# Second attention of a two-layer kernel: side work cut at engine changes, one transposition for the maxima, two engines' sums added before the ones-product

## The chip, the cores and the metric

One Trainium2 chip; the program runs on one of its cores. The metric is the device time of the whole program in microseconds, of which the profile shows one execution.

## The reference, cut to what matters

Two layers on `x` of (4, 512, 256), each a cross attention to a context of 1601 rows and then a mixture of 8 experts. The change is in layer 1: its attention, and the routing of its experts that runs beside it.

```python
# layer 1 attention: h = layernorm(x), 8 heads of 32, keys and values from the context
q = split(h @ Wq.T); k = split(ctx @ Wk.T); v = split(ctx @ Wv.T)
attn = softmax(einsum('bhnd,bhmd->bhnm', q, k) * 32**-0.5)
x = x + merge(einsum('bhnm,bhmd->bhnd', attn, v))
# layer 1 experts: h = layernorm(x)
logits = h @ Wr + br
thresh = top2(logits)[1]
weights = softmax(where(logits >= thresh, logits, -inf))
out = sum_e weights[e] * (gelu(h @ W1[e] + b1[e]) @ W2[e] + b2[e])
x = x + out
```

The shift that a softmax subtracts (the maximum of a row) cancels in the quotient.

## The kernel before, in words

There are four stages in time: the first attention (to about 1577 us), the first experts (to about 1937), the second attention (to about 2606), the second experts (to the end). Every product is float32 on TensorE, and a float32 matmul shows as two records, a transposition as one.

**Second attention.** Its work is cut into 16 units u = (batch b of 4, group o of four heads, half f of the queries), 256 queries of four heads each. A unit has NM = 13 steps j over the 1601 keys, 128 at a time, so step 13u + j; a batch has 52 steps. The outer loop makes an *iteration* of two steps, and writes this order out by hand (`in_order` fixes the order on TensorE, VectorE, ScalarE and GpSimd):

- `weights` of each of the two steps: scores, transposed (keys on partitions), into `ps_w` (L1357), then the exponential on ScalarE into `pT` (L1370). Between the two steps stands one piece of `maxima` of the unit after: scores with queries on partitions into `ps_s` (L1109), and VectorE's maximum of them into `tops` (L1120). A unit has seven such pieces.
- `add_weights` of the two steps before: `sum += pT` (L1379), on GpSimd for j in (1, 4, 7, 10) and on VectorE else, into two sums. Step 0 and step 1 write theirs directly, so GpSimd has three adds per unit and VectorE eight.
- `weigh` of the two steps before: `ps_o += v * pT` (L1388). After the last step of a unit `closing` copies `ps_o` to `oT` (L1400); two iterations later it sums over keys with a product with ones (`ps_n`, L1407, one set of matmuls for each of the two sums); an iteration later it turns `oT` back and divides.
- whatever was put down for these steps by `put`: the side work.

How the maximum gets into the scores: `keyed` and `asked` have 64 rows for a pair of heads, of which 32 hold keys and queries, and one more row of `keyed` holds ones (row 32, and 96 for the other head) while the same row of `asked` holds the negative maxima of the queries. `negated(u)` (L1129) writes them into `shift`, at step 13u-5; `to_row(u)` turns `shift` with four transpositions (L1142) and copies two rows of 512 into `asked` (L1146), at step 13u-4. For an odd u these steps are in one iteration, for an even u in two.

**Side work in this stage.** `collect` gathers the first experts' results for batch b + 1 (8 indirect loads on GpSimd) and `add_collected` adds them; `queries` makes batch b + 1's layer norm and queries; `projected` (batches 1 and 2) makes keys and values of batch b + 1, a piece per iteration, with ScalarE copying them out; `route2(b - 1)` makes the routing of the second experts for the batch before: layer norm, logits, the two chosen experts, their places, the biases' product, and at the end 16 indirect stores ("scatters") of 128 rows of `pay` into `rows_a` and `rows_b` on GpSimd (L535). `queries` and `route2` are generators; each `next` runs one piece. In `ln_root` (L133, L135) VectorE adds the epsilon and ScalarE takes the square root, which takes a table load (and another back to the exponential's).

**Buffers.** `ps_s`, 3 buffers of two banks, serves `ps_w`, the two `ps_s` tiles of a maxima piece and all side work's products; `ps_o` has 1; `ps_m` has 1 and serves `ps_n`, the turned outputs and `ps_r`. `pT` has 6 buffers.

**First experts, second half.** `all_experts(1, keys_next())` calls `next` on the generator `keys_next` twice per expert and once at the end. Its pieces are the projections of batch 1, `queries(0)`, the seven maxima of unit 0, and last `negated(0)` with `to_row(0)`.

**Second experts.** The generator `routing` (`route2(3)` and a table) is called four times per expert tile in `for i in range(E + SURE)`.

Of the kernel before, what the change touches and what calls it, by code (L numbers as in the profile page):

```python
# [16 lines left out]
P = 128  # L17
# [53 lines left out]
def xattn_ffn_twice(ctx: ExitStack, tc: tile.TileContext, a: dict, out: bass.AP):  # L71
# [42 lines left out]
    def ln_moments(pool, src, n, tail=P, mv=None, some=None):  # L114

        if mv is None:
            mv = pool.tile([P, n, 2], F32, tag=f"mv{n}", name="mv")
            if tail < P:
                nc.vector.memset(mv, 1.0)
        for i in some or range(n):  # L120
            r = rows_of(i, n, tail)
            st = pool.tile([P, 6], F32, tag="bnst", name="st")
            nc.vector.bn_stats(st[:r], src[:r, i, :])
            nc.vector.bn_aggr(mv[:r, i, :], st[:r])
        return mv
# [5 lines left out]
    def ln_root(pool, mv, n):  # L131
        ve = pool.tile([P, n], F32, tag=f"ve{n}", name="ve")
        nc.vector.tensor_scalar(ve, mv[:, :, 1], EPS, None, ALU.add)  # L133
        rs = pool.tile([P, n], F32, tag=f"rs{n}", name="rs")
        nc.scalar.activation(rs, ve, AF.Sqrt)  # L135
        return ve, rs
# [62 lines left out]
    in_row = const.tile([P, 1], F32, name="in_row")  # L199
    nc.gpsimd.memset(in_row, 0.0)  # L200
    for r in (32, 96):
        nc.gpsimd.memset(in_row[r : r + 1], 1.0)
# [193 lines left out]
    def route2(b, two, psum, tag, first=0, n=NT):  # L396
# [4 lines left out]
        mv = ln_moments(two, xb, n)  # L401
        root = ln_root(two, mv, n)
        yield
        mv, rs = ln_scale(two, mv, n, root)
        for t in range(n):
            nc.vector.tensor_scalar(
                pay[:, t, :D],
                xb[:, t, :],
                mv[:, t, 0:1],
                rs[:, t : t + 1],  # L410
                ALU.subtract,
                ALU.mult,
            )
            nc.vector.tensor_scalar(
                pay[:, t, D : D + 1], lane, float((b * NT + first + t) * P), None, ALU.add
            )
        xnT = two.tile([P, DC, n * P], F32, tag="xnT2", name="xnT2")
        yield
# [30 lines left out]
        nc.vector.tensor_tensor(wb, lg, top[:, :, 0:1].to_broadcast([P, n, E]), ALU.subtract)  # L449
        nc.scalar.activation(wb, wb, AF.Exp)  # L450
# [5 lines left out]
        nc.vector.tensor_copy(pay[:, :, D + 1 :], wb)  # L456

# [3 lines left out]
        for k in range(2):  # L461
# [7 lines left out]
            chosen.append(ck)  # L469
        mine_b = slice(b * NT + first, b * NT + first + n)  # L470
        nc.vector.tensor_reduce(over[:, mine_b], rest, AX.X, ALU.add)
        nc.vector.tensor_tensor(extra[:, mine_b, :], rest, wb, ALU.mult)

# [3 lines left out]
        for t in range(n):  # L477
            nc.vector.tensor_copy(earlier[:, t, :], taken2)
            nc.vector.tensor_tensor(taken2, taken2, cnt[:, t, :], ALU.add)
        ps = psum.tile([P, n, E], F32, tag=tag, name="ps_c2")  # L480
# [7 lines left out]
        if b == B - 2:  # L488
            nc.vector.tensor_copy(taken_a, taken2)
        for k in range(2):  # L490
            off, place, at, out_of = small("off2"), wide("place"), small("at2"), small("out_of")
            nc.vector.tensor_tensor(place, hot[k], ps, ALU.mult)
# [18 lines left out]
        yield  # L511

        tp = psum.tile([P, 4, P], F32, tag=tag, name="tp_w")
        for t in range(n):
            nc.tensor.transpose(tp[:E, t, :], wb[:, t, :], ident)
        wbT = two.tile([E, n * P], F32, tag="wbT", name="wbT")
        nc.vector.tensor_copy(wbT, tp[:E, :n].rearrange("p i q -> p (i q)"))
        for t0 in range(0, n, 2):
            ps = psum.tile([P, 2, D], F32, tag=tag, name="ps_b2")
            for k in range(2):  # L520
                t = t0 + k
                nc.tensor.matmul(
                    ps[:, k, :], lhsT=wbT[:, t * P : (t + 1) * P], rhs=b2, start=True, stop=True
                )
            xs = xb[:, t0 : t0 + 2, :]
            nc.vector.tensor_tensor(xs, xs, ps, ALU.add)
            yield
# [3 lines left out]
        for rows, at in ((rows_a, place_a), (rows_b, place_b))[b == B - 1 :]:  # L531
            for k in range(2):
                for t in range(n):
                    j = b * NT + first + t
                    nc.gpsimd.indirect_dma_start(  # L535
                        out=rows[:, :],
                        out_offset=bass.IndirectOffsetOnAxis(ap=at[k][:, j : j + 1], axis=0),
                        in_=pay[:, t, :],
                        in_offset=None,
                        bounds_check=E * G - 1 if rows is rows_a else ROWS - 1,  # L540
                        oob_is_err=False,
                    )
                    yield


    with ExitStack() as st:
# [339 lines left out]
        nc.gpsimd.memset(empty, 0.0)  # L886
        with in_order(nc.sync):
            load_second()
# [159 lines left out]
    shift = [soon.tile([P, 2, 2, P], F32, name=f"shift{i}") for i in range(2)]  # L1048
# [3 lines left out]
    def queries(b, qT):  # L1052
        xn = soon.tile([P, NT, D], F32, tag="xn", name="xn")
        mv = ln_moments(turns, x[b], NT)
        root = ln_root(turns, mv, NT)
# [4 lines left out]
        yield  # L1060
# [66 lines left out]
    def negated(u):  # L1127
        for pair in range(2):
            nc.vector.tensor_reduce(  # L1129
                shift[u % 2][:, :, pair, 32::64],  # L1130
                tops[u][:, :, 2 * pair : 2 * pair + 2, :],
                AX.X,
                ALU.max,
                negate=True,
            )
        tops.pop(u)

    def to_row(u):
        ps = banks["m"].tile([P, 2, QH], F32, tag="m", name="ps_r")
        for pair in range(2):  # L1140
            for t in range(2):
                nc.tensor.transpose(  # L1142
                    ps[:, pair, t * P : (t + 1) * P], shift[u % 2][:, t, pair, :], ident
                )
        for r in (32, 96):
            nc.scalar.copy(asked[u % 3][r : r + 1], ps[r : r + 1])  # L1146
# [173 lines left out]
    with ExitStack() as st:  # L1320
# [9 lines left out]

        keyed = [one.tile([P, 2, M], F32, name=f"keyed{o}") for o in range(DC)]
        of_ones = ones[:, 0:1].to_broadcast([P, M])
        for t in keyed:
            nc.scalar.activation(t[:, 0], of_ones, AF.Copy, scale=in_row[:, 0:1])
            nc.vector.tensor_scalar(t[:, 1], of_ones, in_row[:, 0:1], None, ALU.mult)

        def load_keys(b, o):
            for pair in range(2):
                for s in range(2):
# [4 lines left out]
                    )  # L1344

# [27 lines left out]
        def add_weights(u, j, pT):  # L1373
# [5 lines left out]
            (nc.gpsimd if k else nc.vector).tensor_tensor(to, to, pT[:r], ALU.add)  # L1379

# [15 lines left out]
        def closing(u, ps):  # L1396
# [7 lines left out]
            for k in range(2):  # L1404
                for i in range(HG):
# [6 lines left out]
                        stop=k == 1,  # L1412
# [30 lines left out]
        n_units, per_batch = len(units), 4 * NM  # L1443
# [31 lines left out]

        for u in range(1, n_units):
            put(NM * u - 5, lambda u=u: negated(u))
            put(NM * u - 4, lambda u=u: to_row(u))
            put(NM * u - 12, lambda u=u: load_queries(u))
        for b in range(B):  # L1480
            s0 = per_batch * b
            if b:
                put(s0 - 10, lambda b=b: load_keys(b, 0))
                put(s0, lambda b=b: load_keys(b, 1))
                spread(s0 + 10, route2(b - 1, one, ps_s, "s"), 2, 24)
            if b + 1 < B:
# [4 lines left out]
                for t in range(NT):  # L1491
                    put(
                        s0 + 14 + 2 * t,
# [6 lines left out]
                spread(s0 + 22, later(), 2, 5)  # L1500
# [26 lines left out]
        held = []  # L1527
        for step in range(0, NM * n_units + 10, 2):

            fresh = []  # L1530
            for k in range(step, step + 2):
# [3 lines left out]
                if k == step:  # L1535
                    for g in ahead.pop(step // 2, ()):
                        maxima(*g)
            for h in held:
                add_weights(*h)
            for uw, jw, pT in held:  # L1540
                if jw == 0:
# [11 lines left out]
        assert not at and not ahead, (sorted(at), sorted(ahead))  # L1553

# [3 lines left out]
    with ExitStack() as st:  # L1558
# [242 lines left out]
        for i in range(E + SURE):  # L1801
            w, xT, to, share = here
            hT = hidden(w, xT)
            for _ in range(2):
# [5 lines left out]
            next(rest, None)  # L1810
            if last:
                results(*last)
            next(rest, None)
# [131 lines left out]
```

## Time and profile before

| what | value |
|---|---|
| median of 3 runs | 2953.87 us (2949.18 to 2956.38) |
| the profiled execution | 2949.11 us |
| its span | 2947.0 us |
| mean granted TensorE clock | 0.973 |
| second attention, from its first `ps_w` to its last `oT` | 1937.7 to 2598.9 us |
| `pT` exponential, 128x1024, each | 1023 ns |
| VectorE's add, alone, and mean of all | 1222 and 1435 ns |
| GpSimd's add, median | 2372 ns |
| one maxima reduction, 128x1024 | 1217 ns |
| scatter, from issue to landing | 3.0 us (`rows_a`), 2.6 us (`rows_b`) |

Times are of one execution, counted from the span's start. "PE" is TensorE's matmuls, "PEld" its weight loads, DVE VectorE, ACT ScalarE, POOL GpSimd, SP SyncE. In a wait "X <- Y" X stood still until Y ended; in order of time a row has its start, its length, the engine, the line, and in brackets the idle time before it and what ended it. "xN" counts instructions.

### The profile page before, as it was taken

To read this page: it belongs to the slowest core of one execution; us is meant where nothing else is said; L and a number is where in the kernel's file an instruction comes from. 1 tells how busy PE (TensorE), PEld (TensorE's weight loads), DVE (VectorE), ACT (ScalarE), POOL (GpSimd) and SP (SyncE) were. 2 spreads that over 40 slices of the span, in tenths; PEclk is the share of its full clock that TensorE was granted. 3 is DMA by queue.
4 is the path that set the end of the run, shared out by engine and by line. 5 is a ranking of instruction groups with operands and counts; after the bars stand their busy time and mean duration, and the time that the engine had idled before them with its cause. 6 is when DMAs were issued, how large, how long until landed. Compare 5 with 4: busy or idle time off the path is not lost. (4 is left out here: it accounts for less than half of the span.)

```text
span 2947.0 us, 36216 instructions
## 1 busy us (share of the span) xinstructions
PE 2770.3 (94%) x13686; PEld 1883.4 (64%) x13686; DVE 1466.2 (50%) x2333; ACT 937.7 (32%) x1325; POOL 392.5 (13%) x301
## 2 busy tenths in 40 slices
PE   6999999999999999999999799988989898889997
PEld 2666667666766666666666587744444444467886
DVE  6445456544575544454444202267767768742110
ACT  3323334233342333332332112134434344331221
POOL 0000000100001000010000101021314233333442
PEclk9999999999999999999999899999999999999999
DMA  5444443343434333343346798610101021035663
GB/s 162 113 108 113 104 112 85 102 106 92 104 98 109 95 91 92 89 109 94 91 99 185 199 255 235 185 46 16 30 28 48 19 66 63 11 114 154 180 188 82
DMA packets 197448, 314.94 MB, mean 107 GB/s; under 512 B 44007, under 2 KB 118056, under 8 KB 194440
## 3 DMA queue, kind: packets, MB, share of 16 engines
q1 hardware_dynamic: 157512, 227.52, 29.1%
q0 software_dynamic: 15168, 49.23, 5.7%
q10 hardware_dynamic: 24576, 35.68, 4.7%
q8 instruction: 114, 1.87, 0.3%
q14 instruction: 78, 0.64, 0.1%
HBM read 114.64 MB, written 51.86 MB: 56 GB/s over the span
## 5 line engine op out<-in xcount | busy, mean ns | idle before, releaser
L806 DVE TENSOR_REDUCE top<-ps_s 128x1 f32<-128x2113 f32 x128 | 301.9, 2358 | 585.2 <-PE ps_s L798 585.2
L835 PE MATMUL ps_o<-pT,v 128*128 128x256 f32 x2176 | 521.1, 381 | 0.5 <-DVE inv L813 0.5
L798 PE MATMUL ps_s<-kT,qT 128*128 128x512 f32 (+1 forms) x1280 | 488.8, 526 | 6.5 <-ACT attn L812 6.4
L835 PEld LDWEIGHTS ps_o<-pT,v 128*128 128x128 f32 x2176 | 410.0, 191 | 114.5 <-issue 68.3
L812 ACT ACTIVATE attn<-ps_s,top 128x2113 f32<-128x2113 f32 x128 | 258.9, 2023 | 477.5 <-DVE top L806 433.2
L798 PEld LDWEIGHTS ps_s<-kT,qT 128*128 128x128 f32 x1280 | 241.8, 191 | 252.9 <-issue 236.5
L827 DVE STREAM_TRANSPOSE pT<-swapped 128x2176 f32<-128x2176 f32 x128 | 312.4, 2441 | 31.0 <-DMA swapped<-attn 20.4
L1120 DVE TENSOR_REDUCE tops<-ps_s 128x2 f32<-128x1024 f32 (+1 forms) x224 | 238.1, 1105 | 149.6 <-PE ps_s L1109 149.2
L747 PE MATMUL ps_k<-kvin,wkv 128*128 128x512 f32 (+1 forms) x640 | 263.8, 535 | 4.1 <-DVE mv_g L685 2.1
L1357 PE MATMUL ps_w<-asked,keyed 64*128 64x256 f32 (+1 forms) x1664 | 244.7, 416 | 21.1 <-DVE tops L1120 9.6
L781 PE MATMUL ps_v<-wkv,kvin 128*128 128x256 f32 x1088 | 254.6, 381 | 0.7 <-ACT v L788 0.6
L1357 PEld LDWEIGHTS ps_w<-asked,keyed 64*128 64x128 f32 (+1 forms) x1664 | 147.5, 190 | 146.6 <-ACT pT L1370 61.8
L1370 ACT ACTIVATE pT<-ps_w 128x1024 f32<-128x1024 f32 (+1 forms) x176 | 179.3, 1023 | 193.7 <-PE ps_w L1357 191.9
L781 PEld LDWEIGHTS ps_v<-wkv,kvin 128*128 128x128 f32 x1088 | 205.0, 190 | 35.9 <-ACT v L788 6.0
L1379 DVE TENSOR_TENSOR sum<-sum,pT 128x1024 f32<-128x1024 f32 (+1 forms) x128 | 183.2, 1431 | 10.4 <-ACT pT L1370 4.0
L760 ACT ACTIVATE kT<-ps_k,bqk 128x512 f32<-128x512 f32 (+1 forms) x160 | 96.8, 620 | 266.5 <-DMA swapped<-attn 129.0
L1379 POOL TENSOR_TENSOR sum<-sum,pT 128x1024 f32<-128x1024 f32 x48 | 122.6, 2554 | 347.5 <-ACT pT L1370 347.3
L747 PEld LDWEIGHTS ps_k<-kvin,wkv 128*128 128x128 f32 x640 | 116.4, 192 | 78.5 <-issue 67.4
L1109 PE MATMUL ps_s<-kv,qT 32*128 32x512 f32 (+1 forms) x1024 | 135.4, 574 | 14.6 <-ACT kv L1013 6.5
L788 ACT COPY v<-ps_v 128x512 f32<-128x512 f32 x144 | 79.7, 560 | 217.0 <-PE ps_v L781 150.2
L1193 PE MATMUL ps_h<-sxT,w 128*128 128x256 f32 x512 | 116.7, 386 | 2.9 <-ACT hT L1200 2.1
L1207 PE MATMUL ps_y<-w,hT 128*128 128x256 f32 x512 | 114.4, 380 | 0.2 <-DVE y L1215 0.2
(282 smaller groups left out, 2731.5 us busy)
## 6 DMA issues: line engine op xcount, KB each, us to landing
swapped<-attn SPq DMA_DIRECT2D x1536, 68.0 KB, 2.1
swapped<-attn ACTq DMA_DIRECT2D x512, 68.0 KB, 2.2
w<-in_w_dram SPq DMA_DIRECT2D x32, 1024.0 KB, 10.2
rows_b<-empty SPq DMA_DIRECT2D x36, 530.0 KB, 11.3
w_e<-in_wall_dram SPq DMA_DIRECT2D x4, 2052.0 KB, 9.3
cw<-in_ctxT_dram SPq DMA_DIRECT2D x4, 1601.0 KB, 12.5
keyed<-kv SPq DMA_DIRECT2D x32, 200.1 KB, 3.8
ctx_b<-in_ctx_dram SPq DMA_DIRECT2D x3, 1536.0 KB, 8.0
```

The source lines that it names most:

```text
L747: nc.tensor.matmul(ps[:, :n], lhsT=wkv[:, c, hs], rhs=kvin[:, c, : NB - 1, k, :] if k < 4 else kvin[:, c, NB - 1, :, :], start=c == 0, sto ...
L781: nc.tensor.matmul(ps[:, k, :], lhsT=flat_kvin[c][:, j * P : (j + 1) * P], rhs=wkv[:, c, cols], start=c == 0, stop=c == DC - 1,)
L798: nc.tensor.matmul(flat[:, j0 : j0 + n], lhsT=qT[:, t * P : (t + 1) * P], rhs=kT[:, j0 : j0 + n], start=True, stop=True,)
L806: nc.vector.tensor_reduce(top, flat[:, :L], AX.X, ALU.max, negate=True)
L812: nc.scalar.activation(attn[:, :L], flat[:, :L], AF.Exp, bias=top, accum_out=total)
L827: nc.vector.transpose(pT[:, :, k * P : (k + 1) * P].rearrange("p c (a i) -> p a c i", a=4), swapped.rearrange("p a (c i) -> p a c i", i=32),)
L835: nc.tensor.matmul(ps, lhsT=v[:, j - parts[part][0], (h % 2) * DH0 : (h % 2 + 1) * DH0], rhs=pT[:, j, :], start=j == 0, stop=j == NB - 1,)
L1109: nc.tensor.matmul(pss[i // 2][:, i % 2, at : at + n], lhsT=qTs[b][rows, o, q0 : q0 + P], rhs=kvs[b][0][o][rows, j0 : j0 + n], start=True, ...
L1120: nc.vector.tensor_reduce(tops[u][:, t : t + at // n, 2 * pair : 2 * pair + 2, j0 // 512], of, AX.X, ALU.max,)
L1357: nc.tensor.matmul(ps[:r, s, pair * QH : (pair + 1) * QH], lhsT=keyed[o][64 * s : 64 * s + 64, pair, j * P : j * P + r], rhs=asked[u % 3][ ...
L1370: nc.scalar.activation(pT[:r], ps[:r], AF.Exp)
L1379: (nc.gpsimd if k else nc.vector).tensor_tensor(to, to, pT[:r], ALU.add)
```

## The change

- `negated(u)` is one reduction instead of two, at step 13u-7; it writes four columns (32 to 35) in each half of a 128x128 `shift`, in the order query tile, pair. `to_row(u)` at 13u-5 is one transposition and four ScalarE copies of four rows each, which a column of `in_row` scales by one or zero; `keyed` has ones in two of these four rows for each pair. `in_row` is made from four small reductions of the identity.
- At a unit's last step GpSimd adds the second sum to the first (all units but the last), and `ps_n` is one set of matmuls.
- When a unit's last step and the next one's first are in one iteration, `weigh` of the first is put off into the next iteration, ahead of its adds.
- `queries` yields ten times instead of five, `route2` in more places: after each part that another engine goes on with. `wbT` is copied by ScalarE, the counts are copied out of PSUM, and scatters go two to a call, the first four beside the biases' product.
- The steps of the calls are written as lists. `add_collected` starts at 10 instead of 14, `queries` at 12 instead of 22, `route2` at 4 instead of 10.
- The second experts call `routing` eight times per tile.

```diff
-        mv = ln_moments(two, xb, n)
-        root = ln_root(two, mv, n)
+        mv = ln_moments(two, xb, n, some=range(n // 2))
+        yield
+        ln_moments(two, xb, n, mv=mv, some=range(n // 2, n))
+        ve = ln_variance(two, mv, n)
+        yield
+        root = ln_root(two, mv, n, ve)
         yield
         mv, rs = ln_scale(two, mv, n, root)
+        yield
...
+        if b == B - 2:
+            nc.vector.tensor_copy(taken_a, taken2)
+        yield
         ps = psum.tile([P, n, E], F32, tag=tag, name="ps_c2")
...
+        counted = two.tile([P, n, E], F32, tag="counted", name="counted")
+        nc.vector.tensor_copy(counted, ps)
+        tp = psum.tile([P, 4, P], F32, tag=tag, name="tp_w")
...
+        nc.scalar.copy(wbT, tp[:E, :n].rearrange("p i q -> p (i q)"))
+        yield
...
+        def scatters():
+            for rows, at in ((rows_a, place_a), (rows_b, place_b))[b == B - 1 :]:
+                for k in range(2):
+                    for t in range(n):
+                        j = b * NT + first + t
+                        nc.gpsimd.indirect_dma_start(
...
+                        if t % 2:
+                            yield
+        sending = scatters()
         for t0 in range(0, n, 2):
...
+            next(sending)
             yield
...
+        yield from sending
...
     def queries(b, qT):
         xn = soon.tile([P, NT, D], F32, tag="xn", name="xn")
-        mv = ln_moments(turns, x[b], NT)
-        root = ln_root(turns, mv, NT)
+        mv = ln_moments(turns, x[b], NT, some=())
+        for i in range(NT):
+            ln_moments(turns, x[b], NT, mv=mv, some=(i,))
+            if i + 1 < NT:
+                yield
+        ve = ln_variance(turns, mv, NT)
+        yield
+        root = ln_root(turns, mv, NT, ve)
         yield
         mv, rs = ln_scale(turns, mv, NT, root)
         for i in range(NT):
             ln_apply(xn, x[b], mv, rs, i)
-        yield
+            if i in (0, NT - 1):
+                yield
...
     def to_row(u):
-        ps = banks["m"].tile([P, 2, QH], F32, tag="m", name="ps_r")
-        for pair in range(2):
+        ps = banks["m"].tile([P, P], F32, tag="m", name="ps_r")
+        nc.tensor.transpose(ps, shift[u % 2], ident)
+        for r in (32, 96):
             for t in range(2):
-                nc.tensor.transpose(
-                    ps[:, pair, t * P : (t + 1) * P], shift[u % 2][:, t, pair, :], ident
-                )
-        for r in (32, 96):
-            nc.scalar.copy(asked[u % 3][r : r + 1], ps[r : r + 1])
+                nc.scalar.activation(
+                    asked[u % 3][r : r + 4, :, t * P : (t + 1) * P],
+                    ps[r : r + 4].unsqueeze(1).to_broadcast([4, 2, P]),
+                    AF.Copy,
+                    scale=in_row[r : r + 4, 2 + t : 3 + t],
+                )
...
             (nc.gpsimd if k else nc.vector).tensor_tensor(to, to, pT[:r], ALU.add)
+            if j == NM - 1 and merged(u):
+                nc.gpsimd.tensor_tensor(sums[u, 0], sums[u, 0], sums[u, 1], ALU.add)
...
         for u in range(1, n_units):
-            put(NM * u - 5, lambda u=u: negated(u))
-            put(NM * u - 4, lambda u=u: to_row(u))
+            put(NM * u - 7, lambda u=u: negated(u))
+            put(NM * u - 5, lambda u=u: to_row(u))
...
-                spread(s0 + 10, route2(b - 1, one, ps_s, "s"), 2, 24)
+                beside = (4, 8, 10, 18, 20, 22, 24, 28, 30, 32, 34, 36, 38, 40, 42, 44, 46)
+                bare = (4, 8, 10, 12, 14, 16, 18, 20, 22, 24, 26, 28, 30, 32, 34, 36, 38)
+                steps = beside if b + 1 < B else bare
+                place(s0, route2(b - 1, one, ps_s, "s"), (*steps, *range(steps[-1] + 2, 54, 2), *range(54, 62)))
...
-                spread(s0 + 22, later(), 2, 5)
+                place(s0, later(), range(12, 32, 2))
...
             for uw, jw, pT in held:
+                if jw == 0 and held and held[0][:2] == (uw - 1, NM - 1):
+                    late = [(uw, jw, pT)]
+                    continue
```

## The prediction

> **What bounds the kernel now.** I read the page first, then windows, then the waits of TensorE, then order of time. The page says that TensorE is the bound nearly everywhere:
>
> ```profile
> PE 2770.3 (94%) x13686; PEld 1883.4 (64%) x13686; DVE 1466.2 (50%) x2333; ACT 937.7 (32%) x1325; POOL 392.5 (13%) x301
> ```
>
> The second attention runs from about 1937 to 2600 us. Its windows (columns: length, busy PE, PEld, DVE, ACT, POOL, granted clock, DMA share, GB/s):
>
> ```profile
> 2265.00:2306.00 41.00, 39.84 (x352) 19.63 (x354) 33.45 (x42) 19.66 (x24) 20.57 (x15) 1.00 0.15 39
> 2306.00:2347.00 41.00, 32.71 (x235) 19.31 (x228) 29.50 (x81) 14.27 (x19) 4.02 (x2) 0.87 0.08 17
> 2511.00:2552.00 41.00, 33.76 (x258) 18.54 (x258) 28.62 (x80) 11.20 (x15) 11.08 (x6) 0.83 0.05 17
> ```
>
> One stretch runs full at full clock; others lose 7 to 8 us of 41 and have a lower clock besides. Sixteen such windows sum to 583 us of PE in 663. TensorE's own waits in 1937 to 2600 (us in all, times, longest) name the holes:
>
> ```profile
> PE ps_r L1142 <- DVE shift L1129: 17.1, 6, 4.4
> PE ps_w L1357 <- DVE tops L1120: 9.6, 5, 4.6
> PE ps_b L522 <- DVE wbT L517: 8.6, 3, 2.9
> PE ps_c L482 <- DVE earlier L478: 7.6, 3, 2.8
> PE ps_o L1388 <- ACT oT L1400: 7.0, 8, 0.9
> PE ps_s L1109 <- ACT kv L1013: 6.5, 2, 3.3
> ...
> PE ps_c L485 <- DVE earlier L478: 2.3, 3, 0.8
> ```
>
> Behind "tops" and "kv" stands one thing, seen in order of time:
>
> ```profile
> 2489.94 1.28 ACT L135 ACT_TABLE_LOAD   x1
> 2495.23 0.17 DVE L133 TENSOR_SCALAR ve<-mv 128x4 f32<-128x4 f32 x1
> 2495.43 0.21 ACT L135 ACTIVATE rs<-ve 128x4 f32<-128x4 f32 x1 [4.21 <-DVE ve L133]
> 2495.66 1.28 ACT L1370 ACT_TABLE_LOAD   x1
> 2496.58 1.69 PE L1357 MATMUL ps_w<-asked,keyed 64*128 64x256 f32 x8 [4.64 <-DVE tops L1120]
> ```
>
> ScalarE stands with the square root's table until VectorE has got through its queue, the exponentials behind it are late, and TensorE runs out of its three score buffers.
>
> **What the skill says.** TensorE: Matmul & The Clock Gate, Part 1 (the HAM clock gate): an idle window of about 3.4 us halves the clock. The trace agrees: after the 4.40 us wait at 1963.1, eight ps_w records take 2.08 us, elsewhere 1.13. SBUF — State Buffer, "SBUF: two separate sides": a VectorE operation with two SBUF inputs and a GpSimd one that reads SBUF shut each other out. The trace agrees: VectorE's add at 2040.25 takes 3.40 us beside GpSimd's 2.35, alone 1.22. DMA: Bandwidth & Descriptors, "Anatomy of one DMA": most of a transfer's fixed 2 us is the write receipt. The scatters land in 2.6 to 3.0 us, and each next one to the same table waits for that.
>
> **The change part by part**, against the profiled execution, 2949.1 us (span 2947.0 and 2.1 around it; 4.8 below the median shown).
>
> 1. *Maxima a step earlier than their row.* The reduction (L1129) goes to step 13u-7, into the iteration of the last maxima, and the transposition to 13u-5, an iteration on. Of the six waits of L1142 none is left: -17.1.
> 2. *Side work cut at engine changes.* wbT goes to ScalarE and its product a step later; the counts' operands are made a step before: -8.6 -7.6 -2.3. The weighing that waits for the copy of oT is put off by an iteration: -7.0. Together -25.5.
> 3. *Roots.* The variance is made a step before the root, so ScalarE is held for 1.28 + 0.21 + 1.28 = 2.8 us and not 7.0 (2489.94 to 2496.94). The four gaps seen (3.90, 4.64, 3.26, 3.26) sum to 15.1. The exponential behind is still late, so I take half: -8.
> 4. *TensorE's work.* One transposition instead of four: L1142 was busy 10.8 us over 15 units; about half goes, -5.4. One sum instead of two: L1407 was busy 17.9 us, half goes, -8.9. Against it ScalarE writes the row in four instructions of 2x128, not two of 512. The nearest row, gelu 128x256 with a pointer operand, takes 0.84 us for two, so 1.7 instead of 1.16, and the next exponential is that much later. At 2084.79 the trace shows TensorE already meeting it by 0.17 us, so I charge all of it: 15 x 0.54 = +8. Bounds: 0 to +12. Net -6.
> 5. *Clock.* Sixteen windows' (1 - granted clock) x 41 us is 36 us, some of it inside the gaps. After the 3.90 us gap, ps_w, ps_o, ps_w lost 0.85 + 0.86 + 0.95; after the 4.40 us one 1.5. Eleven gaps of over 2.7 us go or get short, 2 us each: -22.
> 6. *Unit 0.* In the expert stage the side work is called 16 + 1 times, and the list before has exactly 17 pieces. `queries` now yields ten times instead of five, so pieces 18 to 22 are never called: maxima 3 to 6 of unit 0, its negation and its row. Its shift stays zero, which leaves the softmax the same as long as exp stays finite. TensorE, full there, loses three groups of 1.14, one of 0.67 and 0.6 of transposing, -4.7, and the row's copy that the next stage waits for (1.26) in part: -5.5.
>
> Gains: 17.1 + 25.5 + 8 + 6 + 22 + 5.5 = 84.
>
> 7. *Scatters.* Before, one scatter per iteration over 16 iterations. Now two per call, and calls at 48, 50, 52, 54, 55, 56, 57, 58: sixteen in six iterations. GpSimd's queue is in order, and each scatter to the same table holds it until the one before has landed:
>
> ```profile
> 2371.88 1.02 POOL L535 DMA_INDIRECT rows_a<-pay,place_a  x1 [0.16 <-issue]
> 2374.60 1.00 POOL L535 DMA_INDIRECT rows_a<-pay,place_a  x1 [1.70 <-DMA rows_a<-pay,place_a]
> 2377.48 0.99 POOL L535 DMA_INDIRECT rows_a<-pay,place_a  x1 [1.88 <-DMA rows_a<-pay,place_a]
> ```
>
> Fourteen of them stand ahead of the next unit's add for j=4. At 2.8 us each, with two adds and a merge in between whose time covers waits, that add ends about 43 us after the first scatter. Its buffer comes round after six tiles: exp j=10 wants it about 39 us after (iterations 5.3, 5.3, 4.4, 4.4, 6.5, 6.6, 6.3 with projections) or 35 without. So about 5 us of stall at steps 114 and 166 and 2 of cold clock each: +14. Bounds: nothing at 2.5 us a scatter, +30 at 3.6. The eight gathers queued there take 1.3 each inside the waits.
> 8. *The tail.* Past step 190 there are no maxima; an iteration is 3.05 us (2568.33, 2571.52, 2574.45). Sixteen scatters fall on steps 196 to 210, ten before the last unit's add j=10, which ends about 33 us after step 196, while its normalization could start at 25: 8 us of waiting in place of today's 4.3 (L1407 at 2598.4): +4.
> 9. *Sums added first.* 15 more GpSimd adds of 2.37 us. Each follows VectorE's last add of the unit; VectorE's next is an iteration later, and TensorE reads the sum two iterations later (8.7 us), so they are hidden: +2 for small VectorE work shut out. Without that cover each costs 2.4, 36 in all.
> 10. *VectorE.* Busy 494 us in these windows. An iteration has 2.36 of maxima and 1.5 of adds against TensorE's 4.33; in the first batch (1937 to 2085) it is busy 118 of 148, and TensorE would now want only about 122. Some stall comes back there: +8 (0 to +20).
> 11. Four small reductions at the start and one more copy (0.2 each) lie under TensorE; the expert stage at the end takes its side work in twice as many calls, with the same instructions: 0 (-5 to +7, its hole of 6.95 us at 2665).
>
> Losses: 14 + 4 + 2 + 8 = 28. Net -56: 2949.1 - 56 = 2893, and on the median's scale **2897 us**.
>
> **Rivals.**
> - *The scatter bursts become the bound.* For: the in-order queue and the landing waits above, with projection loads and first weights moving at the same time. Against: some scatters are shadowed by adds. At 3.6 us a scatter each burst stalls 14 x 1.0 us beyond today's cover, the tail 10: about 30 more: 2925.
> - *VectorE becomes the bound.* For: 118 of a wanted 122 us in the first and last batch, GpSimd's lockouts (its adds average 1435 ns against 1222). Against: full stretches run at 33.5 of 41. It would give back 20 to 25 us: 2920.
> - *Slower.* The same bursts, decided by the scatter interval: at 4.6 us each stalls 14 x 2.0 = 28 us, the tail 20, 76 together, which eats the gain: 2955 to 2965. In the second attention two scatters in a row stand 2.4 to 3.9 us apart where the landing sets it.
> - *Nothing of it* (waits only change names, 2945 to 2960): against it, the waits removed are of TensorE, the full engine, and moving work out of its order leaves only known lags.
>
> **How the numbers follow.** Chances: the forecast 0.60 (its own range 2862 to 2912), bursts 0.17, VectorE 0.13, slower 0.05, nothing 0.05. The range reaches down to all unknown costs at nothing (2897 - 28 = 2869, and some more of the clock) and up through bursts and VectorE together: 2862 to 2938. A measurement of this kernel tells about 0.3% (9 us) from no change. Faster 0.91, same 0.04, slower 0.05.
>
> **What would show it.** Right: no wait of the transposition for the shift; no wait of ps_b, ps_c, ps_o; granted clock near 1.00 in most windows of the stage; ps_n and ps_r with half and a quarter of the records; 40 fewer records of ps_s. Wrong: GpSimd backed up behind scatters around the second and third batch's start, with exponentials waiting for its adds; VectorE over 95% busy; ps_n waiting for the merged sum.

## The result, and the profile after

The changed kernel takes **2978.54 us** (median; 2966.75 to 2985.08), the kernel before beside it 2953.22 (2948.58 to 2956.38). The ratio is 1.0084, 95% interval 1.0062 to 1.0106: slower by 0.84%. Forecast was 2897, range 2862 to 2938. The profiled execution has a span of 2979.5 us against 2947.0.

Where the 32.5 us of span came from, by the starts of the first and last `ps_w` and of the first transposition of the second experts (us):

| part | before | after | difference |
|---|---|---|---|
| start to first `ps_w` of the second attention | 1937.7 | 1944.6 | +6.9 |
| first to last `ps_w` | 658.5 | 666.8 | +8.3 |
| last `ps_w` to the second experts' first transposition | 14.2 | 37.3 | +23.1 |
| from there to the end | 336.6 | 330.8 | -5.8 |

The first and the last row are within the scatter of the runs: in all kernels with the change, which differ little or not at all in these two parts, the second attention begins between 1933.3 and 1947.2 and the last part takes 329.3 to 339.4. The stage and its tail are what changed.

The page after has less work on TensorE, as meant, and about the same on VectorE:

```profile
PE 2760.2 (93%) x13477; PEld 1877.7 (63%) x13477; DVE 1467.7 (49%) x2312; ACT 946.7 (32%) x1357; POOL 418.2 (14%) x313
```

TensorE's waits of 1937 to 2612 (us in all, times, longest), in place of the list shown of before:

```profile
PE ps_w L1403 <- ACT pT L1416: 37.8, 18, 13.1
PE ps_r L1181 <- DVE got L1484: 22.5, 8, 4.6
PE ps_w L1403 <- DVE tops L1162: 16.1, 15, 2.2
PE ps_c L501 <- DVE tops L1162: 8.8, 2, 4.4
PE ps_s L1151 <- DVE tops L1162: 5.3, 3, 4.5
```

None of the old waits on `shift`, `wbT`, `oT`, `kv` is left. New ones, longer, stand in their place: for the exponential, for `got` (the divided outputs), for the slots' counts. Three windows (columns as before: length, busy PE, PEld, DVE, ACT, POOL, granted clock, DMA share, GB/s) show the depth of the holes:

```profile
2222.00:2263.00 41.00, 27.67 (x253) 14.47 (x251) 35.19 (x69) 12.73 (x15) 11.56 (x6) 0.88 0.03 10
2304.00:2345.00 41.00, 27.86 (x199) 15.11 (x197) 24.48 (x30) 14.64 (x20) 23.87 (x16) 0.83 0.15 33
2481.00:2522.00 41.00, 25.55 (x213) 12.41 (x209) 22.51 (x32) 14.00 (x17) 20.02 (x16) 0.79 0.19 70
```

TensorE is busy for 26 to 28 of 41 us; the worst window shown of before had 33. No other engine is full in them either (VectorE, the next, has 35.2 of 41 in the first and less in the others), so these are waits in a chain, and I follow three of them in order of time.

**A, the scatters.** GpSimd at 2304 to 2318, with the exponential (ACT L1416) that waits for it:

```profile
2304.35 1.00 POOL L544 DMA_INDIRECT rows_b<-pay,place_b  x1 [0.89 <-DMA rows_b<-pay,place_b]
2306.71 0.98 POOL L544 DMA_INDIRECT rows_b<-pay,place_b  x1 [1.36 <-DMA rows_b<-pay,place_b]
...
2315.17 2.35 POOL L1425 TENSOR_TENSOR sum<-sum,pT 128x1024 f32<-128x1024 f32 x1
2317.56 1.02 ACT L1416 ACTIVATE pT<-ps_w 128x1024 f32<-128x1024 f32 x1 [12.05 <-POOL sum L1425]
2318.64 2.08 PE L1403 MATMUL ps_w<-asked,keyed 64*128 64x256 f32 x8 [11.62 <-ACT pT L1416]
```

Each scatter to a table waits until the one before has landed; the add for j=4 stands behind ten of them; the exponential wants the `pT` buffer that this add frees; TensorE stands for 11.62 us and begins again at half clock (2.08 us for what takes 1.13). The same happens at 2499.7 (13.12 us). At the end of the stage the scatters run on past the attention:

```profile
2630.18 1.08 PE L1460 MATMUL ps_n<-sum,ones 128*32 128x256 f32 x8 [12.18 <-POOL sum L1425]
...
2643.84 0.98 POOL L544 DMA_INDIRECT rows_b<-pay,place_b  x1 [1.81 <-DMA rows_b<-pay,place_b]
2646.48 3.54 SPq L1672 DMA_DIRECT2D rows<-rows_a  x7
2648.66 1.23 PE L1695 MATMUL tp<-ident,rows 128*128 128x128 f32 x4 [15.62 <-DMA rows<-rows_a]
```

The loads of `rows_a` for the second experts start only after the last scatter. So it was before, but there the sixteen scatters ended with the attention:

```profile
2602.72 1.88 PE L1407 MATMUL ps_n<-sum,ones 128*32 128x256 f32 x16 [4.27 <-DVE sum L1379]
2605.40 0.98 POOL L535 DMA_INDIRECT rows_b<-pay,place_b  x1 [1.74 <-DMA rows_b<-pay,place_b]
2608.13 4.41 SPq L1596 DMA_DIRECT2D rows<-rows_a  x8
2610.42 0.45 PE L1619 MATMUL tp<-ident,rows 128*128 128x128 f32 x1 [4.08 <-DMA rows<-rows_a]
```

**B, one buffer of `ps_m`.** For every even unit, and for the last, the moved transposition now comes right behind the turned outputs:

```profile
2257.36 0.28 PE L1474 MATMUL tp_o<-ident,by 128*128 128x4 f32 x2
2261.45 0.20 DVE L1482 RECIPROCAL inv<-tp_o 128x8 f32<-128x8 f32 x1
2261.69 0.42 DVE L1484 TENSOR_TENSOR got<-tp_o,inv 128x256 f32<-128x256 f32 x1
2262.26 0.45 PE L1181 MATMUL ps_r<-ident,shift 128*128 128x128 f32 x1 [4.62 <-DVE got L1484]
```

`ps_r` and `tp_o` share one buffer. VectorE gets to `tp_o` 3.8 us after it is written, and TensorE, in order, waits.

**C, the merge on GpSimd.** Around the slots' counts:

```profile
2237.73 0.16 DVE L494 COPY earlier<-taken 128x8 f32<-128x8 f32 x1
2237.85 2.37 POOL L1427 TENSOR_TENSOR sum<-sum,sum 128x1024 f32<-128x1024 f32 x1 [14.15 <-DVE sum L1425]
2237.92 2.32 DVE L495 TENSOR_TENSOR taken<-taken,cnt 128x8 f32<-128x8 f32 x1
2240.18 2.33 POOL L1425 TENSOR_TENSOR sum<-sum,pT 128x1024 f32<-128x1024 f32 x1
2240.28 2.27 DVE L494 COPY earlier<-taken 128x8 f32<-128x8 f32 x1
...
2244.74 0.63 PE L501 MATMUL ps_c<-cnt,before 128*128 128x32 f32 x2 [4.42 <-DVE tops L1162]
```

An addition and a copy of eight columns take 2.3 us each instead of 0.17 (the copy ahead of them takes 0.16): as long as GpSimd's adds beside them. The second of these is GpSimd's ordinary next add, which the small operations meet only because the merge has held up the first of them (r2_some below runs without it). The counts come late, TensorE waits 4.42 us.

### The profile page after: what moved, and what is told of

It is laid out like the page before. It is cut to its first block, busy times and chain, and to the rows that moved or that the text cites. A ratio compares the mean times of both kernels' runs of the same rounds, so it can differ in the third digit from the quotient of the medians.

```text
span 2979.5 us, 35818 instructions
## 1 busy us (share of the span) xinstructions
PE 2760.2 (93%) x13477; PEld 1877.7 (63%) x13477; DVE 1467.7 (49%) x2312; ACT 946.7 (32%) x1357; POOL 418.2 (14%) x313
## 5 line engine op out<-in xcount | busy, mean ns | idle before, releaser
L1162 DVE TENSOR_REDUCE tops<-ps_s 128x2 f32<-128x1024 f32 (+1 forms) x216 | 229.8, 1106 | 156.1 <-PE ps_s L1151 155.9
L1416 ACT ACTIVATE pT<-ps_w 128x1024 f32<-128x1024 f32 (+1 forms) x176 | 179.3, 1023 | 232.6 <-PE ps_w L1403 199.3
L1425 DVE TENSOR_TENSOR sum<-sum,pT 128x1024 f32<-128x1024 f32 (+1 forms) x128 | 174.4, 1362 | 8.1 <-ACT pT L1416 4.2
L1151 PE MATMUL ps_s<-kv,qT 32*128 32x512 f32 (+1 forms) x984 | 132.1, 597 | 9.3 <-DVE tops L1162 5.3
```

Source lines behind the costliest of these rows:

```text
L1151: nc.tensor.matmul(pss[i // 2][:, i % 2, at : at + n], lhsT=qTs[b][rows, o, q0 : q0 + P], rhs=kvs[b][0][o][rows, j0 : j0 + n], start=True, ...
L1162: nc.vector.tensor_reduce(tops[u][:, t : t + at // n, 2 * pair : 2 * pair + 2, j0 // 512], of, AX.X, ALU.max,)
L1416: nc.scalar.activation(pT[:r], ps[:r], AF.Exp)
```

## The experiments

Several chips ran these; the kernel before took 2950 to 2953 us (median) on each, but the version without merges took 2893.12, 2904.84 and 2889.17 on three. So differences of under some 15 us are read within a group that shared a chip; the groups are kept together below. The changed kernel itself ran in none of them: a difference from its 2978.54 us is one between groups, so for these the ratios to the kernel before are compared as well.

**First group: theories A, B and C, singly and together.**

```diff
 e1_tables: scatters of a batch take turns between the two tables
-for rows, at in tables:
-    for k in range(2):
-        for t in range(n):
+for k in range(2):
+    for t in range(n):
+        for rows, at in tables:      # two per call, as in the change
```

> The changed kernel with one edit: scatters alternate between the two tables (first to rows_a, second to rows_b, and so on), so that a scatter waits for the landing of the one before last and not of the last. Theory A (GpSimd's queue stands behind scatters that come in a burst): the three long waits of TensorE (11.6 and 13.1 us for exponentials behind GpSimd's adds, 12.2 us for the last unit's sum) shrink to under 3 us each, and the next stage starts 10 to 20 us earlier after the last unit, since the last scatter lands earlier; time 2978 - 40 to - 60, so 2920 to 2940. Theory B (the single buffer that ps_r and the turned outputs share is what costs): hardly any change, over 2970. Theory C (VectorE shut out by GpSimd's adds is what costs): hardly any change.

2941.96 us (2938.88 to 2949.0), ratio to before 0.9969 [0.9957, 0.9982]: 36.6 below the changed kernel (34 by the ratios), a little less than expected. In the profiles the stage is 22.3 us shorter and its tail 15.7. Two scatters in a row are now 1.3 us apart, because neither waits for the other's landing:

```profile
2298.74 0.99 POOL L544 DMA_INDIRECT rows_a<-pay,place_a  x1 [0.31 <-issue]
2300.04 0.98 POOL L544 DMA_INDIRECT rows_b<-pay,place_b  x1 [0.30 <-issue]
...
2302.60 2.35 POOL L1425 TENSOR_TENSOR sum<-sum,pT 128x1024 f32<-128x1024 f32 x1
```

The same ten scatters and five gathers, from 2282.17 to that add, take 20.4 us; in the changed kernel 30.4 (2284.77 to 2315.17). The waits of 11.62 and 13.12 us are gone; the longest wait for an exponential is 1.6. B's waits stand at 22.9, untouched.

```diff
 e2_row
-put(NM * u - 5, lambda u=u: to_row(u))
+put(NM * u - 4, lambda u=u: to_row(u))
```

> The changed kernel with one edit: the row's transposition stands at step 13u-4 as before the change, so that for even u it is an iteration after the turned outputs of the unit before and not right behind them. Theory B (shared buffer): the 8 waits of the transposition for VectorE's reading of the turned outputs, 22.5 us, go, and some 8 us of cold clock with them; time 2978 - 20 to - 30, so 2948 to 2958. Theory A: those waits would only be found again in front of the bursts; over 2970.

2957.17 us (2953.0 to 2967.32), ratio 1.0026 [1.0015, 1.0037]: 21.4 below the changed kernel (17 by the ratios). The waits of `ps_r` fall from 22.5 us to 0.35; those for the exponential stay (longest 10.7).

> Both edits together. If A and B are separate causes the gains add: 2978 - 60 to - 85, so 2893 to 2918, faster than the kernel before. If VectorE is the bound behind them (theory C), less than two thirds of the sum of the two single gains.

e3_both has both edits: 2922.18 us (2915.01 to 2928.04), ratio 0.9911 [0.9894, 0.9927]. 56.4 below the changed kernel, where the two alone sum to 58.0 (51 and 51 by the ratios): the gains add, so A and B are separate, and VectorE isn't the next bound behind them, which was expected to keep back a third or more.

```diff
 e4_nomerge: as e3_both, and
 def merged(u):
-    return u + 1 < n_units
+    return False               # TensorE sums both halves again
```

> Both edits, and GpSimd's add of the two sums taken out again: the product with ones runs over both sums in every unit, as before the change. TensorE gets 15 x 0.49 = 7 us more work. Theory C (VectorE shut out by GpSimd): the waits of the counts' product for maxima (8.8 us) and part of the waits for maxima (16 us) go, so 0 to 10 us faster than with the merge. If the merge is hidden: 5 to 8 us slower than with it.

2893.12 us (2889.89 to 2893.36), ratio 0.9802 [0.9786, 0.9818]. C was expected to be worth up to 10 us; against e3_both, on the same chip, it is 29, although TensorE does more. The next group asks why.

**Second group: what about the merge costs.** Beside these ran e8_unit0, which belongs to another step.

```diff
 e5_vector: as e3_both, and
-nc.gpsimd.tensor_tensor(sums[u, 0], sums[u, 0], sums[u, 1], ALU.add)
+nc.vector.tensor_tensor(sums[u, 0], sums[u, 0], sums[u, 1], ALU.add)
```

> The scatters by turns to two tables and the row at 13u-4 stay; the sum of the two sums is made on VectorE, right behind its own last add, and not on GpSimd. TensorE keeps its one-sum normalization. Theory C, that the merge costs 29 us net because it stands on GpSimd (it waits there at the head of the queue for VectorE, and shuts VectorE's small additions and copies out while it runs): the two waits of ps_c, 4.42 each, and the half clock behind them go, and the time is near that of the version without a merge, 2885 to 2902. Rival, that VectorE has no room for 15 more adds of 1.2 us, or that the earlier end of the sum alone does the harm: 2910 to 2930, with more waits for tops.

2916.43 us (2915.32 to 2929.13), ratio 0.9897 [0.9872, 0.9922]: the rival's figure, no gain over GpSimd. The trace shows one reason, and it is the shut-out again:

```profile
2216.12 1.23 DVE L1427 TENSOR_TENSOR sum<-sum,sum 128x1024 f32<-128x1024 f32 x1
...
2218.38 2.37 POOL L1425 TENSOR_TENSOR sum<-sum,pT 128x1024 f32<-128x1024 f32 x1 [16.36 <-ACT pT L1416]
2218.58 2.20 DVE L494 COPY earlier<-taken 128x8 f32<-128x8 f32 x1
...
2222.17 0.41 PE L501 MATMUL ps_c<-cnt,before 128*128 128x32 f32 x2 [3.53 <-DVE tops L1162]
```

The merge makes VectorE's chain of small operations 1.2 us later, and so it runs into GpSimd's ordinary next add. This doesn't exclude the rival, that VectorE has no room: TensorE's other waits for `tops` are 22.8 us here against 18.4 in e3_both.

```diff
 e6_late: as e3_both, the merge taken out of add_weights, and in the loop, at closing
+if merged(uw):
+    at.setdefault(step + 2, []).insert(0, lambda uw=uw: merge(uw))
```

> As the version with both changes, but the merge on GpSimd is issued an iteration later, when VectorE's last add is long done: it no longer stands at the head of GpSimd's queue waiting. If the harm is the waiting (adds, scatters and gathers behind it come late): 2895 to 2905. If the harm is the shut-out of VectorE's small operations while it runs: another iteration's small operations are hit, the waits for ps_c may go or may turn up at another tile, and the time stays between 2910 and 2930.

2919.86 us (2917.19 to 2920.61), ratio 0.9892 [0.9875, 0.9908]. Inconclusive as a test of the waiting. The trace has the merge at 2222.14, right behind VectorE's last add (2220.79 to 2222.00), 0.12 us after the first small copy, as in the version with both edits. GpSimd had no other instruction in between, so an iteration later in the written order was no later in time.

```diff
 e7_only_merge: the changed kernel, and
 def merged(u):
-    return u + 1 < n_units
+    return False
```

> The changed kernel with nothing undone but the merge: two sums go to TensorE again, scatters and row as the change has them. If the merge's cost is its own (shut-out and cold clock after 4.4 us waits), 2978 falls by about 29, to 2945 to 2955. If it is part of the scatter bursts' cost (the merge queued among them), the gain here is larger, 2925 to 2945, since the bursts are still there. If the gain appears only when the bursts are gone: 2965 to 2980.

2947.26 us (2942.91 to 2955.06), ratio 0.9985 [0.9978, 0.9993]: by the ratios 1.0% or some 29 us below the changed kernel, with the bursts and B left in. The merge costs as much with the bursts as without them. Part of it here goes by way of the bursts, because the merge waits at the head of GpSimd's queue ahead of them: without it the stall at the third batch's start is 3.88 us instead of 11.62, and the tail is 7.9 us shorter; the other stall stays, at 13.57.

```diff
 e8_unit0: as e4_nomerge, in keys_next
-for _ in queries(0, qTs[0]):
-    yield
+for i, _ in enumerate(queries(0, qTs[0])):
+    if i in (4, 6, 7, 8, 9):
+        yield
```

> The version without a merge, and the queries of the first batch's side list take five pieces again and not ten, so that all maxima of unit 0, its negated maxima and its row are made. The forecast's step 6 put what had been left out at 5.5 us: 2893 becomes 2897 to 2900. Rival: the 17th piece, the maxima that now stand at the very end of the list and make TensorE wait 4.5 us at 1931, goes back under the experts, and the time stays the same or falls by up to 5: 2886 to 2893.

The first batch's queries are five pieces again: 2896.26 us (2886.91 to 2903.02), ratio 0.9804 [0.9781, 0.9827]. Against 2893.12 on another chip this tells nothing of an effect of 5 us in either direction.

```diff
 e9_some: as e3_both, no merge in the unit that closes beside the counts
-    return u + 1 < n_units
+    return u + 1 < n_units and u % 4 != 2
```

> As the version with both changes and the merge on GpSimd, but without the merge in the four units of which the closing falls into the iteration of the slots' counts (every fourth unit, from the third on; their normalization takes two sums). Where the merge stood, a 128x8 addition and a 128x8 copy took 2.33 and 2.27 us and TensorE waited 4.42 us for the counts, twice, with half clock behind it. If the shut-out at this one place is what the merge costs, most of the 29 us comes back: 2922 becomes 2896 to 2906, no ps_c wait over 1 us. If the merge costs a little in all 15 units: a quarter comes back, 2912 to 2918.

2904.18 us (2900.63 to 2908.28), ratio 0.9834 [0.9812, 0.9856]: 16 below e6_late, which ran on the same chip with all merges.

```diff
 e10_before_tables: the kernel before, and
-for rows, at in tables:
-    for k in range(2):
-        for t in range(n):
+for k in range(2):
+    for t in range(n):
+        for rows, at in tables:      # one per call, as it was
```

> The kernel before, with nothing changed but the order of its scatters: by turns to the two tables, one for each call as before. If the landing waits of GpSimd (30.3 and 24.6 us there) were hidden because the scatters stood one to an iteration, nothing happens: 2945 to 2957. If changing tables is a gain of its own, outside the bursts: 2935 or less.

2951.47 us (2944.55 to 2954.95), ratio 0.9994 [0.9984, 1.0004]. Nothing. Changing tables is no gain of its own; while scatters stand one to an iteration their landing is hidden.

**Third group.** e12_again is e4's kernel once more.

```diff
 e11_quiet: as e3_both, no merge in the third and fourth unit of a batch
-    return u + 1 < n_units
+    return u + 1 < n_units and u % 4 < 2
```

> The merge on GpSimd left out in two more of every four units than in none: it stays in the first and second unit of a batch, and is left out in the third (slots' counts) and in the fourth (where it stands in GpSimd's queue ahead of the scatters, waiting for VectorE up to 12.6 us, and the exponential of a later tile waits 4.56 us for an add behind them). If that queue is the rest of the merge's cost, the 4.56 us wait goes and 2904 becomes 2890 to 2897, the level of the version without any merge or 2 to 4 below it. If the rest is spread over all merges: 2899 to 2904.

> The version without any merge once more, beside the one above: 2888 to 2898.

2911.04 us (2910.43 to 2916.12), ratio 0.9866 [0.9847, 0.9886], and 2904.84 us (2902.76 to 2911.16), ratio 0.9842 [0.982, 0.9865]. The 4.56 us wait that e9 still had is gone, and yet e11 was not faster than no merge. e4's kernel is 12 us above its first time, and some 9 of them go with the clock: its mean granted clock is 0.976 here and was 0.979 there (0.981 in r4_nomerge below). Why it differs is open. So the groups couldn't be subtracted, and four versions ran on one chip.

**Fourth group: all merges, three quarters, half, none.** The kernels are those of e3_both, e9_some, e11_quiet and e4_nomerge.

> Scatters by turns, row at 13u-4, all 15 merges on GpSimd: 27 us above the version without merges on the same chip if the clock there behaves as on the first chip, 15 to 20 if as on the last.

> No merge in the third unit of each batch, where it meets the counts. If the counts are where the cost lies: at least 12 us below the version with all merges. If every merge costs alike: 4 to 7 below.

> No merge in the third and fourth unit of each batch. If the queue ahead of the scatters costs the rest: 6 to 10 us below the one before, and within 3 of the version without merges. If not: within 3 of the one before.

> No merges: 2890 to 2906, the lowest of the four by 0 to 10 us.

| version | us (lowest to highest) | ratio to before |
|---|---|---|
| r1_both, all 15 | 2917.64 (2915.77 to 2926.11) | 0.9886 [0.9871, 0.9901] |
| r2_some, none at the counts | 2897.32 (2896.49 to 2898.53) | 0.9819 [0.9806, 0.9832] |
| r3_quiet, half | 2895.47 (2893.68 to 2903.41) | 0.9816 [0.9801, 0.9830] |
| r4_nomerge, none | 2889.17 (2887.29 to 2892.51) | 0.9792 [0.9778, 0.9805] |

20.3 of the merge's 28.5 us lie at the counts, a place that a batch passes once. In r1's trace four of the 128x8 operations there take 2.3 us; in those of r2, r3 and r4 none takes over 0.5. Without the merge the first eight of them in r2 run from 2217.83 to 2219.42 and are done before GpSimd's next add begins at 2220.17. The step from three quarters to half (1.8) is within the scatter of the runs, so the queue ahead of the scatters, my idea for the rest, isn't shown; the last 6.3 is not located.

How do two waits of 4.42 us make 20? The windows behind the first of them in r1_both say it:

```profile
2223.00:2227.00 4.00, 0.68 (x16) 0.13 (x4) 3.79 (x8) 0.32 (x1) 2.87 (x2) 0.99 0.00 0
2227.00:2231.00 4.00, 2.83 (x12) 2.02 (x14) 3.41 (x4) 0.57 (x1) 0.00 (x0) 0.50 0.00 0
2231.00:2235.00 4.00, 3.88 (x30) 2.56 (x28) 1.65 (x3) 1.02 (x1) 0.00 (x0) 0.50 0.01 4
2235.00:2239.00 4.00, 4.00 (x40) 1.85 (x40) 1.84 (x12) 1.53 (x3) 0.00 (x0) 0.73 0.00 0
```

The clock is halved from 2227 to 2237. TensorE is busy for nearly all of that from 2228 on, so this hole of 4.42 us costs 4 to 5 us more behind it; the other one, of 4.41, is followed by as much. Summed from the first to the last `ps_w` (waits: TensorE's over 0.15 us; clock lost: half of the time at half clock, and how much of that fell while TensorE was busy, the rest being inside waits that are counted already):

| version | first to last `ps_w` | waits | clock lost | of it, TensorE busy | to the second experts |
|---|---|---|---|---|---|
| before | 658.5 | 70.1 | 35.6 | 33.6 | 14.2 |
| after | 666.8 | 90.4 | 51.7 | 38.6 | 37.3 |
| e1_tables | 644.5 | 71.5 | 39.2 | 34.4 | 21.5 |
| e2_row | 638.8 | 68.0 | 39.3 | 31.1 | 37.2 |
| r1_both | 623.7 | 52.0 | 32.9 | 31.1 | 22.1 |
| r2_some | 606.0 | 50.1 | 13.6 | 12.2 | 15.9 |
| r4_nomerge | 601.1 | 41.5 | 12.4 | 12.1 | 16.5 |

From r1 to r2 the stage is 17.7 us shorter, the sum of waits hardly changes (52.0 and 50.1: other short waits take the place), and TensorE loses 18.9 us less to the clock while it is busy. The half clock around the two holes, 10.2 us at each, makes some 9 of these; the rest went at other places, some of them without a long wait. One profile is no exact measure of this: the version without merges lost 8.5, 12.4 and 21.0 us of clock in its three profiles. But all runs of r1 have a mean granted clock of 0.972 or 0.973 and all of r2 one of 0.977 to 0.980, which over 2900 us makes about 19.

A hole has no fixed price. In the kernel before, 3.4 us of half clock followed the waits of 4.40 and 4.64 us; in r1 3.4 followed one of 4.56 and 10.2 each those of 4.41 and 4.42. In the stage every stretch of half clock is 3.4 us long or a multiple of that, up to 17.1 in the changed kernel. Nor does it take a long hole: in r1 6.8 us of half clock began at 2250.8, and no wait in the 7 us before was longer than 1.3. What decides the length isn't shown.

**r4_nomerge is the best version**: the change without the merge, with scatters in turns and the row at 13u-4, 2.1% below the kernel before here and 2.0 and 1.6% on the two other chips.

## Why the prediction was wrong

The three causes, taken away together, bring the changed kernel from 2978.54 to 2889.17, 61 us below before: as a sum the gains were there, and the losses ate them. What failed are the terms for the bursts and the tail (+14 and +4 forecast), the merge (+2) and the row's transposition (no loss forecast): taken away one at a time they gave 36.6, 31.3 and 21.4 us (34, 29 and 17 by the ratios). By its steps:

- **1, the maxima: wrong.** "Of the six waits of L1142 none is left" holds of the waits for `shift`. But the step counted only what the transposition waits *for*, not the buffer it writes *to*: at 13u-5 it shares an iteration with the turned outputs in `ps_m`'s one buffer. In place of 17.1 us of waits came 22.5 at the same instruction. Putting the row back alone: -21.4.
- **2, side work: mostly right.** The waits of `ps_b` and `ps_o` are gone. The one of `ps_c` came back as 8.8 us by way of the merge.
- **3, roots: right** in that the four gaps of 3.26 to 4.64 us are gone; the many short waits for `tops` rose (`ps_w` 9.6 to 16.1 us in all, though two of those gaps had been in the 9.6).
- **4, TensorE's work: right.** `ps_n` fell from 256 to 136 records and 19.8 to 11.6 us busy, `ps_r` from 60 to 15 and 10.8 to 5.1. The row's four ScalarE copies take 1.66 us, forecast 1.7.
- **5, the clock: wrong in sign.** Forecast -22; the clock lost rose from 35.6 to 51.7, and from 33.6 to 38.6 counted only while TensorE was busy. It was worked out as if long gaps only went away. Without A, B and C it is 12.4, about the forecast's gain, so 2 us a gap suited the old gaps; behind a new one of 4.42 it was 4 to 5. TensorE: Matmul & The Clock Gate, Part 1 (the HAM clock gate), puts the return to full clock after at least one busy window of about 3.4 us; here that was a lower bound: the half clock lasted 10.2 us, and TensorE was busy for 8.8 of them. Nor did the clock fall only after 3.4 us of waiting, as the prediction had it: in the trace before, half clock began around waits of 2.79 us too (at 2230.8, 2343.4 and 2415.1).
- **6, unit 0:** 40 records of L1151 fewer, as said (1024 to 984). The 5.5 us can't be seen: the first `ps_w` came 6.9 us later, but that start varies by 14 us among kernels that do the same up to there. One maxima piece of unit 0 now stands at the very end of the experts, and TensorE waits 4.51 us there (2.75 before). e8 couldn't size it.
- **7, the bursts: right mechanism and place (steps 114 and 166), size wrong.** Forecast 5 us of stall at each, measured 11.62 and 13.12. At step 114 the add ended 60 us after the first scatter, not 43 (2257.45 to 2317.52). Of the 17 us, 11 are GpSimd standing at the head of its queue for an exponential (6.88) and, at the merge, for VectorE's add (4.10) before the last ten scatters; these were taken as cover that costs nothing. The ten stood 3.1 us apart on average, not 2.8: the gathers did not fit inside the waits.
- **8, the tail: wrong.** 8 us forecast for `ps_n`, 12.18 measured; and the step overlooked that the loads of the second experts come after the last scatter: TensorE waits 15.62 us for them, before 4.08. The tail's 23.1 us are most of the 32.5.
- **9, the merge: wrong, and the largest misjudgement of a "hidden" cost.** "VectorE's next add is an iteration later" is true, but VectorE's small operations stand right there. I allowed 2 us for them; the merge costs 28.5 net in r1 against r4. What was missed is in SBUF — State Buffer, "Who interferes with whom": a copy can take the shared port pair as well, and the loser waits for the whole instruction. The trace agrees: 2.27 us for a 128x8 copy beside GpSimd's 2.33. Where the last 6.3 us of the merge go isn't known.
- **10 and 11:** VectorE's busy time is the same (1466.2 and 1467.7). In the first 150 us of the stage TensorE's short waits for `tops` rose from 0.7 to 5.6 us, where 8 more were forecast. The 5.8 us of the second experts are within the scatter. None of these decides.

Of the rivals, the one that ended slower (2955 to 2965) named the bursts, decided at 4.6 us a scatter. The sign was right and the condition wrong: in the ten before the late add they stood 2.4 to 3.9 us apart, and the bursts and the tail, taken away by e1, account for 36.6 of the 89 us. Of the three signs named for a wrong forecast the first came, GpSimd backed up behind scatters with exponentials waiting for its adds. Of the second there was a neighbour: `ps_n` waited for GpSimd's sum, but in the last unit, which has no merge. The third, VectorE over 95% busy, did not come. The figure of the bursts' rival is off by itself: worked out as the slower one's was, 2 x 14 + 10 us in place of the 18 forecast, it is 2917 and not 2925.

## What to carry to other kernels

For an instruction that is moved, list what else uses the buffer that it writes and what stands ahead of it on its engine at the new place, not only what it reads. Stores in a row to one tensor, issued from an engine whose queue also holds arithmetic, cost their landing time each (here 2.4 to 3.9 us); spread them out, as the kernel before did, or take turns between tensors. An add put on an idle engine isn't free: look at what the engine that shares its ports does in those microseconds, and price a hole of over 4 us on TensorE above its length: here one of 4.4 us cost 1.7 us more in the kernel before and 4 to 5 in r1.

## What the runs showed of the hardware that I had not expected

- An operation of eight columns (128x8) takes 2.2 to 2.3 us instead of 0.17 when a GpSimd add of 128x1024 runs beside it.
- Writing an instruction later in an in-order queue moved it by nothing in time, where nothing else stood in that queue.
- Half clock outlasted a hole of 4.42 us by 9 us of nearly full work in one place; in another, after one of 4.40 us, it lasted 3.4.
- One program's time differed by 0.5% between three chips (2889.17 to 2904.84) on which the kernel before agreed within 0.1%; the granted clock differed with it.
